# A two-layer network in one kernel: TensorE's instructions of the recurrence in an order written by hand

## The chip, the core and the metric

The kernel runs on one core of a Trainium2 chip. The time is that of one execution on the device, in microseconds (us), from the first to the last instruction of the program and what lies around them; smaller is better. The engines are TensorE (PE in the profile, with its weight loads as PEld), VectorE (DVE), ScalarE (ACT), GpSimd (POOL) and SyncE (SP), whose queue issues nearly all DMAs.

## The reference

The input is two sequences of 1024 tokens of 256 values, in float32. Each block's result is added to its input and a layer norm follows:

```python
x = _layernorm(x + _L0_attn_ref(x, ...))   # causal attention with rope, 32 query heads, 8 key heads
x = _layernorm(x + _L0_ffn_ref(x, ...))    # gated FFN with int8 weights, 1024 hidden
x = _layernorm(x + _L1_attn_ref(x, ...))   # gated delta rule, 16 heads of 128
x = _layernorm(x + _L1_ffn_ref(x, ...))    # FFN with weights sign(w), relu, 1024 hidden
```

The change touches the third line. There q, k and v are each a projection, a causal convolution over four tokens and a SiLU, and a state S of 128 x 128 per head goes from token to token:

```python
def step(S, inp):
    qt, kt, vt, at, bt = inp
    err = jnp.einsum('bhvk,bhk->bhv', S, kt) - vt
    S = at[..., None, None] * S - bt[..., None, None] * err[..., None] * kt[:, :, None, :]
    o = jnp.einsum('bhvk,bhk->bhv', S, qt)
    return (S, o)
```

Then o is normalised per head, multiplied with sigmoid(x @ Wg), and projected with Wo.

## The kernel before

Attention and most of the first FFN fill the first 690 us or so. The third line is done by `delta_rule`, with the rest of the first FFN at its start and the last FFN at its end.

**Units.** The 2048 tokens are four halves of 512 (`hi`), each in four chunks of 128 (`c`). The 16 heads are eight pairs (`s`). A *unit* `i` is one pair of heads in one half; there are 32. Inside a chunk the recurrence is solved at once: a triangular matrix `lt` of each chunk is inverted ahead, and then only the step from chunk to chunk is serial.

**Parts of a unit**, each a Python generator that writes some instructions and then yields a weight:

- `keys(i)` (four units ahead): projection of k for each of the two heads (`project`, six matmuls into one of the two banks of the PSUM pool `ps_p`; `mm3`, lines 790 to 792), the convolution `conv` (bias on ScalarE, L209; three terms on VectorE, L216; SiLU, L223), the scan of the decay (L247) and k times k (`pkk`, L253, into `lt`, L254).
- `blocks(n)` (for two units at once): forward substitution of the 16 x 16 diagonal blocks in 15 steps of two VectorE instructions (L297, L300), a copy (L302), a write to DRAM and eight loads back (L310), a transpose on VectorE (L313).
- `levels(n)`: the inverse is built up from blocks of 16 to 32, 64 and 128 by small matmuls (`p0`, `px`, `p1`, `p2`, `p3`, `p4`: lines 325 to 380), each with a copy on VectorE or ScalarE to the next.
- `others(i)` and `rest_of(i)` (one unit ahead): q and v as k above, the transpose of k (`pk`, L395, to `kc`, L397), k times q (`pkq`, L404, L405), decays multiplied in on GpSimd (L416, L417), and the projection and tanh of the gate (L422).
- `recur(i)`: the chain. Per chunk: `pr` (L517, L521), copied to `prs` on ScalarE (L523); `pw` (L529), copied to `wc` (L531); `pm` (L541), from which VectorE makes the next state `M` (L547, L545), that the next `pr` needs; and `po` (L554, L555), copied to `o` (L558).
- `finish(i - 1)` (the tail): normalise o (L438 to L452), transpose it (`pt`, L458, into the one bank of the pool "t"), gate it (L460, `y` L461), split it on GpSimd (L464, L740), project it (`pf`) and add it to the tokens (L478).
- `last_ffn`, from unit 29 on: the last FFN (L619 to L658), matmuls `ph` (L633, L634) and `po` (L644).

**Order.** `merge` takes, for each unit, the parts that belong to its stage, and always goes on with the one whose yielded weights are least, as a share of the part's total (`KEYS`, `OTHERS`, `RECUR`, ...). What is written so is not yet the order on the engines: a scheduler goes through the program with its own model of times, and gives each engine the ready instruction that was written first; only dependencies are kept. `blocks` is written whole at the start of its stage, and a step of the tail follows each step of the chain.

Of the kernel before, what the change touches and what calls it, by code (L numbers as in the profile page):

```python
# [20 lines left out]
P = 128  # L21
# [10 lines left out]
HP = 2  # L32
# [51 lines left out]
KEYS, OTHERS, FIRST_OTHERS, RECUR, GATES, LEVELS, TAIL = 9.685, 11.658, 15.197, 12.328, 3.1, 24.4, 1.711  # L84
FFN0, FFN1, FFN1_LAST, FFN1_TAIL = 15.0, 2.0, 8.0, 1.0
LEVEL_STEPS = 7.0, 1.5, 1.5, 3.0, 1.7, 2.7, 0.509, 2.908


def delta_rule(
    tc, a, w1d, xs, ident, load_tokens, store_tokens, mm3, sub_low, rsqrt, layernorm, open_pool, gx, gates, halves,  # L90
    before, out, up_scale, down_scale,
# [111 lines left out]
    def conv(m, i, h, bufs):  # L203
# [3 lines left out]
        pp = project(m, i, h)  # L207
# [18 lines left out]
    def keys(i):  # L226
# [6 lines left out]
        dec = [decay(hi, s * HP + h, 0, "da") for h in range(HP)]  # L233
        for h in range(HP):
            conv("k", i, h, 10)
            if h == 0 and i < last:
                st[i + 1]["wk"] = weights("k", place(i + 1)[1])
            yield 1.3
        for h in range(HP):
# [11 lines left out]
            for c in range(HC):  # L251
                t = slice(c * P, (c + 1) * P)
                nc.tensor.matmul(pkk[:, t], lhsT=k[:, t], rhs=k[:, t], start=True, stop=True)  # L253
# [4 lines left out]
            yield 1.1  # L258
# [17 lines left out]
    def blocks(i, psum):  # L276
# [16 lines left out]
        for j in range(SB - 1):  # L293
# [7 lines left out]
            yield 0.3  # L301
# [14 lines left out]
    def levels(i, psum):  # L316
# [5 lines left out]
        with tc.high_priority():  # L322
            for v in range(2 * U):
                for r in quarter:
                    nc.tensor.matmul(p0[r, v, :], lhsT=lo[r, v, :], rhs=dd[r, v, :], start=True, stop=True)
# [6 lines left out]
        with tc.high_priority():  # L332
            for v in range(2 * U):
                for r in quarter:
                    nc.tensor.matmul(px[r, v, :], lhsT=dt[r, v, :], rhs=n0[r, v, :], start=True, stop=True)
# [13 lines left out]
        with tc.high_priority():  # L349
            for v, lt, u in us:  # L350
                nc.tensor.matmul(p1[b1, v, :], lhsT=lt[b0, u, b1], rhs=X[b0, v, 0:BL], start=True, stop=True)
                nc.tensor.matmul(p1[b3, v, :], lhsT=lt[b2, u, b3], rhs=X[b2, v, 0:BL], start=True, stop=True)
# [5 lines left out]
        with tc.high_priority():  # L358
            for v, lt, u in us:
                nc.tensor.matmul(p2[b0, v, :], lhsT=n1[b1, v, :], rhs=lt[b1, u, b1], start=True, stop=True)  # L360
                nc.tensor.matmul(p2[b1, v, :], lhsT=lt[b1, u, b1], rhs=n1[b1, v, :], start=True, stop=True)
                nc.tensor.matmul(p2[b2, v, :], lhsT=n1[b3, v, :], rhs=lt[b3, u, b3], start=True, stop=True)
# [6 lines left out]
        for n in range(2):  # L369
            p3 = bank(*psum, "p3").rearrange("p (u t) -> p u t", t=64)  # L370
            with tc.high_priority():
                for v, lt, u in us[n * U : (n + 1) * U]:
                    nc.tensor.matmul(p3[Z, u, :], lhsT=lt[A, u, Z], rhs=X[A, v, :], start=True, stop=True)
# [4 lines left out]
            with tc.high_priority():  # L378
                for v, lt, u in us[n * U : (n + 1) * U]:
                    nc.tensor.matmul(p4[A, u, :], lhsT=n3[Z, u, :], rhs=lt[Z, u, Z], start=True, stop=True)  # L380
# [3 lines left out]
    def others(i):  # L384

        for m in "qv":
            for h in range(HP):
                conv(m, i, h, 4)
                yield 1.3
        for h in range(HP):  # L390
            e, k, q = st[i]["at", h], st[i]["k", h], st[i]["q", h]
            pk = bank(ps_m, "m", "pk")
            for c in range(HC):
                t = slice(c * P, (c + 1) * P)
                nc.tensor.transpose(pk[:, t], k[:, t], ident)  # L395
# [4 lines left out]
            st[i]["kc", h] = kc  # L400
            pkq = bank(ps_m, "m", "pkq")
            for c in range(HC):
                t = slice(c * P, (c + 1) * P)
                nc.tensor.matmul(pkq[:, t], lhsT=k[:, t], rhs=q[:, t], start=True, stop=True)  # L404
            nc.vector.scalar_tensor_tensor(e, pkq, -SCALE, e, ALU.mult, ALU.mult)  # L405
            yield 1.3

    def rest_of(i):
# [4 lines left out]
        for h in range(HP):  # L413
# [4 lines left out]
            yield 0.2  # L418
        for h in range(HP):
            pp = project("g", i, h)  # L420
            g = half_tile(pools["late"], "gt", 5)
            nc.scalar.activation(g, pp, AF.Tanh, scale=0.5)  # L422
            st[i]["gt", h] = g
            yield 1.3

    def finish(i, wo, o, chunks):
# [26 lines left out]
        yield 0  # L453
        ys = []
        for h in range(HP):
            pt = bank(pools["t"], "t", "pt")[:, 0 : nc_ * P]
            for c in chunks:
                nc.tensor.transpose(pt[:, (c - c1) * P : (c - c1 + 1) * P], o[:, c, h, :], ident)  # L458
# [8 lines left out]
            yield 0.45 * nc_ / HC  # L467
        for c0 in range(0, nc_, 2):
            pf = bank(pools["t"], "t", "pf").rearrange("p (c e) -> p c e", e=E)
            for c in range(2):  # L470
# [4 lines left out]
                if c == 0:  # L475
                    yield 0.87
# [5 lines left out]
            yield 0.87  # L482
# [5 lines left out]
    def recur(i):  # L488
# [13 lines left out]
        def tail():  # L502
            while tails:
                w = next(tails[0], None)
                if w is not None:
                    return w
                tails.pop(0)
            return 0.0

        lt = st[i]["lt"]  # L510
        o = pools["late"].tile([P, HC, HP, P], F32, name="o", tag="o")
        for c in range(HC):
            t = slice(c * P, (c + 1) * P)
            pr = bank(pools["c"], "c", "pr")
            for h in range(HP):
                r = slice(h * P, (h + 1) * P)
                nc.tensor.matmul(  # L517
                    pr[:, r], lhsT=st[i]["v", h][:, t], rhs=ident, start=True, stop=(M is None), is_transpose=True
                )
                if M is not None:  # L520
                    nc.tensor.matmul(pr[:, r], lhsT=st[i]["k", h][:, t], rhs=M[:, r], start=False, stop=True)  # L521
            prs = pools["late"].tile([P, HP * P], F32, name="prs", tag="prs")
            nc.scalar.copy(prs, pr[:, 0 : HP * P])  # L523
            yield 0.65
            yield tail()
            pw = bank(pools["c"], "c", "pw")
            for h in range(HP):
                r = slice(h * P, (h + 1) * P)
                nc.tensor.matmul(pw[:, r], lhsT=lt[:, h * HC + c, :], rhs=prs[:, r], start=True, stop=True)  # L529
            wc = pools["late"].tile([P, HP * P], F32, name="wc", tag="wc")  # L530
            nc.scalar.copy(wc, pw[:, 0 : HP * P])  # L531
            yield 0.45
            yield tail()
            Mn = None
            if hi % 2 == 0 or c < HC - 1:
# [3 lines left out]
                for h in range(HP):  # L539
                    r = slice(h * P, (h + 1) * P)  # L540
                    nc.tensor.matmul(pm[:, r], lhsT=st[i]["kc", h][:, c, :], rhs=wc[:, r], start=True, stop=True)  # L541
# [9 lines left out]
            for h in range(HP):  # L551
                r = slice(h * P, (h + 1) * P)
                if M is not None:
                    nc.tensor.matmul(po[:, r], lhsT=st[i]["q", h][:, t], rhs=M[:, r], start=True, stop=False)  # L554
                nc.tensor.matmul(  # L555
                    po[:, r], lhsT=st[i]["at", h][:, t], rhs=wc[:, r], start=(M is None), stop=True
                )
# [4 lines left out]
            yield 1.3  # L562
            yield tail()
# [7 lines left out]
    def last_ffn():  # L571
# [29 lines left out]
        for j, (hi, c0, nc_) in enumerate(pieces):  # L601
# [10 lines left out]
            for n in range(0, nc_, 2):  # L612
# [4 lines left out]
                for k in range(2):  # L617
                    for i in range(2):
                        nc.tensor.transpose(  # L619
                            pt[:, k, i * P : (i + 1) * P], x[:, c0 + n + i, k * P : (k + 1) * P], ident  # L620
                        )
# [6 lines left out]
            for f in range(NF + 1):  # L628
                if f < NF:
                    ph = bank(ps_p, "p", "ph")[:, w_]  # L630
                    for k in range(2):
                        w = up[2 * k + f // 4][:, f % 4 * P : (f % 4 + 1) * P]
                        nc.tensor.matmul(ph, lhsT=w, rhs=xh[:, k, w_], start=(k == 0), stop=False)  # L633
# [816 lines left out]
```

## Time and profile before

| | |
|---|---|
| median of three timed runs | 2095.18 us (2093.09 to 2097.55) |
| profiled execution | 2099.4 us |
| its span | 2097.7 us |
| matmuls busy | 1905.9 us, 91% |
| weight loads busy | 1498.2 us, 71% |
| VectorE busy | 1611.1 us, 77% |
| ScalarE busy | 1131.9 us, 54% |
| GpSimd busy | 762.8 us, 36% |
| mean granted TensorE clock | 0.973 |

The span runs from the first to the last instruction; the 1.7 us beside it lie around the program. "Busy" is the time that an engine's instructions cover. Matmuls overlap, so that a new one starts before the last has ended, and a busy TensorE may still have room. Records of fp32 matmuls come as two passes each. A line of the profile names the engine, the line of the kernel, and the tile written and those read.

### The profile page before, as it was taken

To read this page: it belongs to the slowest core of one execution; us is meant where nothing else is said; L and a number is where in the kernel's file an instruction comes from. 1 tells how busy PE (TensorE), PEld (TensorE's weight loads), DVE (VectorE), ACT (ScalarE), POOL (GpSimd) and SP (SyncE) were. 2 spreads that over 40 slices of the span, in tenths; PEclk is the share of its full clock that TensorE was granted. 3 is DMA by queue.
4 is the path that set the end of the run, shared out by engine and by line. 5 is a ranking of instruction groups with operands and counts; after the bars stand their busy time and mean duration, and the time that the engine had idled before them with its cause. 6 is when DMAs were issued, how large, how long until landed. Compare 5 with 4: busy or idle time off the path is not lost.

```text
span 2097.7 us, 48705 instructions
## 1 busy us (share of the span) xinstructions
PE 1905.9 (91%) x18656; PEld 1498.2 (71%) x18656; DVE 1611.1 (77%) x3878; ACT 1131.9 (54%) x2349; POOL 762.8 (36%) x1217
## 2 busy tenths in 40 slices
PE   4989999999988887899999999999999999999996
PEld 2545555555555786788888888888888888787885
DVE  5756666877747996587788878888898888978587
ACT  2355566576655345555555555655564565555543
POOL 1243333331123322144363443444345344344331
PEclk9899999999999899999999999999999999999999
DMA  7454443442132421443444444443444343443110
GB/s 222 144 164 144 144 131 126 142 134 68 51 75 61 133 64 35 127 126 91 119 121 115 124 118 115 107 120 107 121 131 119 113 118 107 137 118 107 32 41 31
DMA packets 313514, 230.90 MB, mean 110 GB/s; under 512 B 139649, under 2 KB 278657, under 8 KB 313281
## 3 DMA queue, kind: packets, MB, share of 16 engines
q1 hardware_dynamic: 299472, 210.80, 34.6%
q10 hardware_dynamic: 9632, 10.76, 1.6%
q0 software_dynamic: 4176, 6.23, 1.2%
q8 instruction: 147, 2.41, 0.5%
q14 instruction: 87, 0.70, 0.1%
HBM read 172.95 MB, written 51.87 MB: 107 GB/s over the span
## 4 chain that ended last, share of the span: by engine, by line
PE 50%; DVE 19%; ACT 6%; DMA 5%; issue 4%; SPq 1%; POOL 1%; POOLq 0%; DVEq 0%; ACTq 0%
PE pp L790 4%; PE pp L792 4%; PE pp L791 4%; PE ps L1110 4%; PE av L1131 3%; PE ps L1058 3%; DVE q L216 2%; PE pkq L404 2%; DVE at L247 2%; PE pw L529 2%; PE pm L541 2%; DVE k L216 2%; PE pkk L253 2%; PE po L555 2%; PE p L380 2%
## 5 line engine op out<-in xcount | busy, mean ns | idle before, releaser
L1067 DVE TENSOR_REDUCE mx<-ps 128x4 f32<-128x1024 f32 (+1 forms) x320 | 344.7, 1111 | 133.5 <-PE ps L1058 91.9
L1114 ACT ACTIVATE es<-ps 128x512 f32<-128x512 f32 (+1 forms) x608 | 314.8, 577 | 135.3 <-PE ps L1110 128.7
L1110 PE MATMUL ps<-qT,kT 128*128 128x512 f32 (+3 forms) x768 | 221.1, 369 | 17.9 <-ACT es L1114 15.8
L1058 PE MATMUL ps<-kT,qT 128*128 128x512 f32 x576 | 203.2, 428 | 23.3 <-DVE mx L1067 16.9
L1110 PEld LDWEIGHTS ps<-qT,kT 128*128 128x128 f32 x768 | 130.9, 189 | 106.2 <-ACT es L1114 53.7
L216 DVE SCALAR_TENSOR_TENSOR k<-pp,cw,k 128x511 f32<-128x511 f32 (+2 forms) x192 | 141.8, 740 | 31.0 <-ACT k L209 19.9
L1058 PEld LDWEIGHTS ps<-kT,qT 128*128 128x128 f32 x576 | 102.5, 194 | 85.7 <-DVE mx L1067 51.9
L1131 PE MATMUL av<-es,vaug 128*32 128x512 f32 (+3 forms) x1536 | 161.7, 501 | 0.0
L216 DVE SCALAR_TENSOR_TENSOR v<-pp,cw,v 128x511 f32<-128x511 f32 (+2 forms) x192 | 141.2, 738 | 13.1 <-ACT halos L213 8.5
L416 POOL TENSOR_TENSOR q<-q,dg 128x512 f32<-128x512 f32 x64 | 82.2, 1285 | 184.5 <-ACT pt L460 31.6
L216 DVE SCALAR_TENSOR_TENSOR q<-pp,cw,q 128x511 f32<-128x511 f32 (+2 forms) x192 | 139.2, 733 | 11.0 <-ACT q L209 9.4
L740 POOL TENSOR_TENSOR wfl<-wf,wfh 128x256 fp32r<-128x256 f32 x80 | 58.4, 733 | 208.3 <-ACT wfh L828 165.2
L1117 POOL TENSOR_SCALAR_AFFINE_SELECT es<-es 128x512 f32<-128x512 f32 x128 | 80.3, 636 | 146.9 <-ACT es L1114 146.7
L529 PE MATMUL pw<-prs,lt 128*128 128x128 f32 x512 | 84.8, 288 | 23.4 <-ACT prs L523 23.3
L555 PE MATMUL po<-wc,at 128*128 128x128 f32 x512 | 98.4, 279 | 2.1 <-ACT wc L531 1.2
L763 POOL TENSOR_TENSOR om<-om 128x8 f32<-128x8 f32 x93 | 20.3, 218 | 213.7 <-DVE om L756 113.8
L529 PEld LDWEIGHTS pw<-prs,lt 128*128 128x128 f32 x512 | 70.7, 194 | 33.2 <-ACT prs L523 29.7
L558 ACT COPY o<-po 128x256 f32<-128x256 f32 x128 | 47.6, 372 | 79.3 <-PE po L555 78.4
L242 POOL TENSOR_SCALAR_AFFINE_SELECT d<-col 128x512 f32<-128x512 f32 x64 | 51.2, 812 | 105.6 <-DVE at L247 96.7
L554 PE MATMUL po<-M,q 128*128 128x128 f32 x448 | 87.6, 278 | 0.0
L828 ACT CAST wfh<-wf 128x256 fp32r<-128x256 f32 x80 | 32.3, 406 | 101.6 <-DMA wf<-in_w1k 28.6
L531 ACT COPY wc<-pw 128x256 f32<-128x256 f32 x128 | 47.5, 371 | 72.7 <-PE pw L529 71.7
(305 smaller groups left out, 5646.1 us busy)
## 6 DMA issues: line engine op xcount, KB each, us to landing
da<-dec SPq DMA_DIRECT2D x64, 256.0 KB
wk<-w1k SPq DMA_DIRECT2D x64, 256.0 KB
wq<-w1q SPq DMA_DIRECT2D x64, 256.0 KB
wv<-w1v SPq DMA_DIRECT2D x64, 256.0 KB
dg<-dec SPq DMA_DIRECT2D x64, 256.0 KB
wg<-w1g SPq DMA_DIRECT2D x64, 256.0 KB
wo<-w1o SPq DMA_DIRECT2D x64, 256.0 KB
ad<-avs ACTq DMA_DIRECT2D x32, 256.0 KB
```

Of the source, the lines that this page charges most:

```text
L216: nc.vector.scalar_tensor_tensor(acc[:, d:], pp[:, 0 : HT - d], cw[:, n, hd, KS - 1 - d : KS - d], acc[:, d:], ALU.mult, ALU.add)
L529: nc.tensor.matmul(pw[:, r], lhsT=lt[:, h * HC + c, :], rhs=prs[:, r], start=True, stop=True)
L554: nc.tensor.matmul(po[:, r], lhsT=st[i]["q", h][:, t], rhs=M[:, r], start=True, stop=False)
L555: nc.tensor.matmul(po[:, r], lhsT=st[i]["at", h][:, t], rhs=wc[:, r], start=(M is None), stop=True)
L790: nc.tensor.matmul(out, lhsT=lhi, rhs=rhi, start=k0, stop=False)
L791: nc.tensor.matmul(out, lhsT=lhi, rhs=rlo, start=False, stop=False)
L792: nc.tensor.matmul(out, lhsT=llo, rhs=rhi, start=False, stop=k1)
L1058: anchor["mm"] = nc.tensor.matmul(ps[:, j - j0, :].rearrange("p (g k) -> p g k", k=P), lhsT=q_, rhs=kT[:, :, j * P : (j + 1) * P], start=T ...
L1067: nc.vector.tensor_reduce(mx[:, it, j0 // 2, :], ps[:, 0:n, :].rearrange("p j (g k) -> p g j k", k=P), AX.XY, ALU.max)
L1110: nc.tensor.matmul(ps[:, g - g0, :], lhsT=kT[:, g, jb * P : (jb + 1) * P], rhs=qT[:, i0 : i0 + w], start=True, stop=True,)
L1114: exps.append(nc.scalar.activation(es[:, g0 : g0 + n, 0:w], ps, AF.Exp, scale=D ** -0.5))
L1131: mm = nc.tensor.matmul(av[ROW * g : ROW * (g + 1), i0 - ih * 512 : 512], lhsT=vaugs[b][:, jb, kv, :], rhs=es[:, g, 0:w], start=(jb == 0), ...
```

## The change

TensorE's instructions are linked, each to the one before, by a dependency that costs no semaphore, from unit 0 on; so TensorE runs them in the order in which they were written. All weights are now shares of a stage, set so that each step of a part comes at a chosen place. `merge` keeps the chain apart: after a step of it, at least four instructions of TensorE from other parts are written before its next one, if there are any. Both heads are projected one right behind the other, before their convolutions. `pk` comes ahead of q and v in `others`. The tail is a part of its own, and `blocks` too, its 15 steps spread over the stage.

```diff
-KEYS, OTHERS, FIRST_OTHERS, RECUR, GATES, LEVELS, TAIL = 9.685, 11.658, 15.197, 12.328, 3.1, 24.4, 1.711
-FFN0, FFN1, FFN1_LAST, FFN1_TAIL = 15.0, 2.0, 8.0, 1.0
-LEVEL_STEPS = 7.0, 1.5, 1.5, 3.0, 1.7, 2.7, 0.509, 2.908
+GATES, TAIL = 3.1, 0.4
+FFN0, FFN1, FFN1_LAST, FFN1_TAIL = 7.6, 2.0, 8.0, 1.0
+LEVEL_STEPS = 0.2, 0.1, 0.04, 0.15, 0.075, 0.13, 0.045, 0.08
+class InLine:
+    def __init__(self, tc):
+        self.tc, self.strict, self.last, self.count = tc, False, None, 0
+    def link(self, made):
+        if self.strict and self.last is not None:
+            self.tc.add_manual_dep(
+                made.ins, self.last.ins.name,
+                mybir.DependencyInfo(mybir.DependencyClass.NoSync, mybir.DependencyReason.DATA), reason="order",
+            )
+        self.last = made
+        self.count += 1
+        return made
...
     def keys(i):
...
+        yield 0.04
+        pps = [project("k", i, h) for h in range(HP)]
+        if i < last:
+            st[i + 1]["wk"] = weights("k", place(i + 1)[1])
         for h in range(HP):
-            conv("k", i, h, 10)
-            if h == 0 and i < last:
-                st[i + 1]["wk"] = weights("k", place(i + 1)[1])
-            yield 1.3
+            conv("k", i, h, 10, pps[h])
+        yield 0.36
...
     def blocks(i, psum):
...
-            yield 0.3
+            yield 0.06
...
     def others(i):
-        for m in "qv":
-            for h in range(HP):
-                conv(m, i, h, 4)
-                yield 1.3
+        yield 0.12
         for h in range(HP):
...
+        yield 0.15
+        for m in "qv":
+            pps = [project(m, i, h) for h in range(HP)]
+            for h in range(HP):
+                conv(m, i, h, 4, pps[h])
+            yield 0.25 if m == "q" else 0.17
...
     def rest_of(i):
...
+        yield 0.04
+        pps = [project("g", i, h) for h in range(HP)]
         for h in range(HP):
-            pp = project("g", i, h)
...
     def recur(i):
...
             nc.scalar.copy(prs, pr[:, 0 : HP * P])
-            yield 0.65
-            yield tail()
+            yield 0.09
...
             nc.scalar.copy(wc, pw[:, 0 : HP * P])
-            yield 0.45
-            yield tail()
+            yield 0.08
...
-            yield 1.3
-            yield tail()
+            yield 0.08
...
-    def merge(parts, aside=None):
+    def merge(parts, aside=None, chain=None):
...
+        held = None
+        if chain:
+            chain = [*chain, 0.0, True]
+            parts.append(chain)
         while any(p[3] for p in parts):
-            p = min(parts, key=lambda p: p[2] / p[1])
+            free = [p for p in parts if not (p is chain and held is not None and te.count < held + 4)]
+            p = min(free or parts, key=lambda p: p[2] / p[1])
...
+            if p is chain:
+                held = te.count
...
     for i in range(-AHEAD, last + 1):
+        te.strict = i >= 0
...
         if n % 2 == 1 and 3 <= n <= last:
-            drain(blocks(n - 1, (pools["l"], "l")))
+            parts.append((blocks(n - 1, (pools["l"], "l")), 1.0))
...
+        if i >= 0 and tails:
+            parts.append((rest(), 1.0))
...
-        merge(parts, aside)
-    for t in tails:
-        merge([(t, TAIL)], (ffn1, FFN1_TAIL))
+        merge(parts, aside, (recur(i), 1.0) if i >= 0 else None)
+    merge([(rest(), TAIL)], (ffn1, FFN1_TAIL))
```

Every `nc.tensor.matmul` and `nc.tensor.transpose` is passed to `te.link`; `rest()` runs the tails that are open. The weights of `finish` are shares now too, and two of its yields are gone.

## The prediction

> **What bounds the kernel now.** I read the page's head first, then the table by stages, then the list of waits, then the timeline around one drop of the clock. All times are those of the profiled execution: 2099.4 us, of which the span is 2097.7; the three timed runs have a median of 2095.2, so a saving is taken off both alike.
>
> The page's head, share of the span and the granted clock:
>
> ```profile
> PE 1905.9 (91%) x18656; PEld 1498.2 (71%) x18656; DVE 1611.1 (77%) x3878; ACT 1131.9 (54%) x2349; POOL 762.8 (36%) x1217
> ...
> PEclk9899999999999899999999999999999999999999
> ```
>
> TensorE leads, VectorE is second, and the two stand close. The first `prs` copy (L523) of unit 1 starts at 887.0 us and that of unit 28 at 1897.2: 27 units in 1010.2 us, a pitch of 37.4 us. The change keeps TensorE's order up to about 830 us almost as it was, so those 32 units (some 1200 us) and the last FFN behind them are all that it can move. Two units out of the table by stages (a line is: stretch, its length, busy time of PE, PEld, DVE, ACT, POOL, clock, DMA share, GB/s), and the sum over units 1 to 20:
>
> ```profile
> 1373.90:1411.00 37.10, 35.14 (x536) 31.09 (x534) 30.61 (x76) 21.52 (x46) 17.21 (x30) 1.00 0.43 119
> 1411.00:1446.80 35.80, 35.14 (x361) 31.61 (x362) 29.15 (x83) 19.54 (x46) 14.02 (x25) 1.00 0.43 117
> ...
> sum 749.50, PE 708.38 PEld 625.32 DVE 620.23 ACT 418.84 POOL 320.56; mean PE 35.42 PEld 31.27 DVE 31.01 ACT 20.94 POOL 16.03
> ```
>
> A unit has 35.4 us of busy TensorE and 31.0 of busy VectorE in 37.5. Starts show more room than "busy" does: in the chain of waits 128x512 projections start 0.233 us apart, 128x128 passes 0.112, transposes 0.109, 128x256 passes 0.118. A unit's 48 projections, 107 passes, 24 transposes and 24 `pf` make 11.2 + 12.0 + 2.6 + 2.8 us, and half of a pair's substitution levels some 4.2 (four groups of 1.07 and some 4 us of smaller ones in each pair): an estimate of 32.8 us. So no order makes a unit shorter than about 33 us; VectorE's 31 us lie just below.
>
> What TensorE waited for between 900 and 1930 us (27.5 units), total, times, longest:
>
> ```profile
> PE pw L529 <- ACT prs L523: 14.0, 23, 1.6
> PE pm L541 <- ACT wc L531: 9.3, 20, 0.7
> PE pp L790 <- DVE q L216: 7.1, 12, 1.4
> PE p L373 <- ACT lt L368: 4.0, 4, 1.6
> PE p L360 <- ACT n L356: 3.9, 4, 2.5
> PE pr L517 <- DVE M L547: 3.3, 1, 3.3
> PE pp L790 <- DVE k L216: 3.2, 5, 0.9
> ```
>
> All rows of this list make 55 us, 2.0 us a unit, 64 us over 32 units. That is the pot. The two first rows are the chain: `pr` to `prs` to `pw`, `pw` to `wc` to `pm`, each with a 0.372 us copy on ScalarE between.
>
> **The change, part by part.** Counts of instructions are the same on every engine: 12,318 matmuls are written in both. Only places change.
>
> *Chain steps at fixed places.* In the new order, 12 projections (12 x 0.233 = 2.8 us) stand between most `pr` and their `pw`. The need is the last pass 0.275 + copy 0.372, and at worst one bias activation ahead in ScalarE's queue (L209, 0.78): 1.4 us. So the 14.0 us go. Between `pw` and `pm` stand 8 transposes (0.87), one `pkk` (0.90) or 12 `pf` (1.4 us), against the same 0.65 to 1.4: half of 9.3 + 1.2 (the `po` row on `wc`) goes, 5.2. That is 19.2 us over 27.5 units, 22 over 32. If the cover were gone, the old 1.0 us a unit would be back.
>
> *Substitution spread.* The 15 steps (L297, L300: 41.4 + 43.2 us for 14 pairs of units, 6.0 us a pair) no longer stand at the head of a stage but between the convolutions. `p1` to `p2` now has `pr` and a projection pair between (3.5 us) against two `n1` of 0.59 behind eight copies of 0.40; `p2` to `p3` has 4.1 us against 0.68 + 4 x 0.36. So the 4.0 and 3.9 us go: 9 us over 32 units. What may be late next is the step after it: the last row is copied (L302), then written out and read back by eight loads on SP's queue; that chain took 8.7 us once (1229.6 to 1238.3), and the new order leaves 11.7 us from the `g` projections to `p0` (2.8 + `pw` 0.45 + `pf` 1.41 + `po` 0.9 + `pr` 0.67 + 2.8 + `pw` 0.45 + `pk` 0.87 + `pm` 0.45 + `po` 0.9). SP's queue holds the same loads, in some pairs with `wo`, which waits for `pf`, among the eight. 3.0 us of cover: I take nothing, and at worst the same 3.0 for each of 14 pairs (+42).
>
> *Both heads' projections together.* Two PSUM banks hold them. The second head's six matmuls come 1.4 us after the first's, and wait until VectorE has done the third convolution term of the previous pair's second head. In VectorE's new order there stand, between the two third terms, in an even unit: `kc` 0.68, two `M` 0.68, a `k` term 0.74, two statistics 0.56, three normalisations 1.16 and the last term 0.74: 4.6 us of durations. So the wait may be up to 4.6 - 1.4 = 3.2 us where VectorE is behind. Below, all the present 10.3 us (`pp` on `q` and `k`) could go, -12 over 32 units; above, 3.2 in each of 16 even units, +51. The nearest row is the present wait for the same bank, 0.6 us at a time: I take no change, 0.
>
> *Fixed places behind VectorE.* `pt` of the second head waits for the only bank of its pool, that is for `y` of the first (L461), which VectorE's queue holds behind the `q` convolution. Between the two `pt` stand 2.7 us of TensorE's work; the need is 0.75 (L460) + 0.68, or, if all six terms of 0.74 are still ahead, 4.4 + 0.7. Below, the present 1.1 us goes, -1; above, 4.4 + 0.7 - 2.7 = 2.4 us a unit, +77. Nearest row: 1.1 us in 27.5 units; with nothing to pull ahead I take 0.1 a unit, +3.
>
> *The last FFN.* A block is four `ph` and four `po` (L644), 8 x 0.233 = 1.86 us. In the new order the `po` of a block stand right behind the next four `ph` (0.93 us), and need relu 0.69 + copy 0.53 + difference 0.93 = 2.15 after their own. Taken by turns this gives (1.86 + 2.15) / 2 = 2.0 us a block, 0.15 more; with POOL's difference (1.28) 2.18, 0.32 more. About 20 such blocks stand behind the chain: +3; below 0, above +6. 54 more of its matmuls (12.6 us) stand behind the chain's end than now; the last three units lose the same work.
>
> Sum: -22 - 9 + 0 + 3 + 3 = -25 us. Profiled 2099.4 - 25 = 2074; median 2095 - 25 = **2070**.
>
> Two rules of the Trainium skill bear on this. The trace has a clock of 0.50 in stretches of 3.4 or 6.8 us; one:
>
> ```profile
> 1486.00:1492.70 6.70, 4.61 (x42) 4.06 (x41) 6.61 (x19) 3.71 (x10) 0.00 (x0) 1.00 0.69 220
> 1492.70:1499.50 6.80, 6.80 (x29) 5.26 (x29) 4.10 (x22) 2.19 (x5) 2.32 (x12) 0.50 0.25 81
> ```
>
> It came when TensorE had been busy 4.61 of 6.70 us, with one wait of 1.6 in it; a stretch costs half its length, 3.4 us. "TensorE: Matmul & The Clock Gate", Part 1 (the HAM clock gate), says that the clock falls to half after an idle window of some 3.4 us; the row shows it after less. By the rule, waits of at most 3.2 us would cost no clock; by the row, one in each pair of units would cost up to 14 x 3.4 = 48 us more, which speaks against the change. Second, "Trainium Kernel Development and Optimization", Performance Expectations, calls busy matmul time a bad measure and LDWEIGHTS time a good one: here 625.3 of 749.5 us, so by it 17% of a unit, 200 us over 32, would be room; the list of waits has 64.
>
> **Rivals.** *Slower: in-order TensorE behind VectorE.* Everything behind a waiting matmul waits too, and the scheduler no longer pulls other work ahead. For it: VectorE's 31 us in a unit of 33, and the bank wait of 3.2 us above. Against: in the present order the same banks cost 10 us in all. If it strikes in the 16 even units, 16 x 3.2 = 51 us, less 31 saved, +6 of the two small terms: +26, about 2121. It decides from 31 / 32 = 1 us a unit.
> *Large gain.* All 64 us of waits go, and VectorE's 31 us stay hidden: 2095 - 64 = 2031; against it, VectorE then would be busy 31 of 35.4.
> *No change.* The waits only change their names: the chain's 1 us a unit returns as waits for banks. 2095.
>
> **How the numbers follow.** Chances: forecast 0.40 (2050 to 2085), large gain 0.18, no change 0.08 (within 0.2%, 4 us, about what a measurement can tell here), slower 0.34. Faster 0.58. The range takes in the large gain with a little of the half clock's return (2020) and the slower case with a part of both upper bounds (51 + 77, half of it, less 31): 2128, so 2130. What lies above needs both at once, or SP's 42 us.
>
> **What the new profile would show.** Right: the rows of `pw` on `prs` and `p` on `n` and `lt` gone, a pitch near 36.6 us, VectorE at 31 us a unit. Wrong: `pp` waiting for L216 or `pt` for `y` by more than 30 us in all, the clock at 0.50 more often than now (five stretches between 900 and 1930), or VectorE waiting for the loads of `dt`.

## The result, and the profile after

The changed kernel takes 2206.3 us (median of four runs, 2197.6 to 2208.1), the kernel before beside it 2096.3 us: a ratio of 1.0519, interval 1.0488 to 1.0550. The forecast of 2070 us and its range up to 2130 us were wrong. The profiled execution took 2208.1 us, its span is 2206.4.

Line numbers have moved: the convolution's term L216 is now L232, the projections L790 to L792 are L817 to L819, `pt` L458 is L482, `y` L461 is L485, the chain's copies L523 and L531 are L537 and L544, the substitution's L297 is L316 and the copy into its bank L292 is L311. The head of the page after:

```profile
PE 1937.2 (88%) x18656; PEld 1515.4 (69%) x18656; DVE 1596.7 (72%) x3878; ACT 1144.6 (52%) x2349; POOL 760.8 (34%) x1217
...
PEclk8999999999998998999999999999989999999998
```

The work is the same. TensorE is busy 31 us longer than before, and the span is 109 us longer, so most of the loss is TensorE standing still. Cut at the first `prs` copies of units 0 and 28, it divides so:

| stretch | before, us | after, us | loss | TensorE idle, before and after |
|---|---|---|---|---|
| span's start to unit 0 | 836.5 | 846.6 | 10.1 | |
| unit 0 to unit 28 | 1060.7 | 1110.8 | 50.1 | 63.7, 107.2 |
| unit 28 to the end | 200.5 | 249.0 | 48.5 | 23.7, 49.3 |

In the middle, what TensorE waited for between 880 and 1960 us (total, times, longest):

```profile
PE pp L817 <- DVE k L232: 53.0, 33, 2.5
PE pt L482 <- DVE y L485: 15.4, 12, 3.2
PE pr L535 <- DVE M L557: 9.1, 8, 2.9
PE pr L535 <- DVE M L559: 7.4, 7, 2.2
PE pm L553 <- ACT wc L544: 5.1, 7, 0.9
PE pw L542 <- ACT prs L537: 2.1, 2, 1.4
```

The two rows that led before, 14.0 and 9.3 us on ScalarE's copies, now stand at the foot with 2.1 and 5.1. Above them are new rows, all on VectorE. The largest, a projection that waits for a bank which the key convolution still reads, had 3.2 us in the list of before.

The table by stages shows where. An odd stage (unit 17's), then an even one (unit 18's), columns as in the prediction:

```profile
1509.00:1554.90 45.90, 41.32 (x681) 36.02 (x680) 31.54 (x87) 25.84 (x58) 13.85 (x24) 0.96 0.48 134
1554.90:1590.00 35.10, 31.25 (x206) 28.14 (x205) 30.35 (x92) 16.77 (x38) 14.57 (x25) 0.95 0.43 113
```

Stages are no longer alike. An odd one has the levels of a pair of units (681 matmul records against 206), an even one the substitution on VectorE. Over units 2 to 27 TensorE is busy 41.4 us in an odd stage and 30.7 in an even one, at 45.3 and 34.7 us a stage; before it was 35.9 and 35.0, at 37.9 and 37.4. VectorE is busy 31.1 and 30.6 us of a stage. In all gaps of over 0.15 us ahead of `pp` from 846 to 1957 us (55.3 us), 48.4 lie in even stages, nearly all at two places, 6.7 and 10.6 us after the stage's start. Both seen in TensorE's timeline of unit 18, in brackets the idle time before an instruction:

```profile
1559.39 0.61 PE L567 MATMUL po<-wc,at 128*128 128x128 f32 x4
1561.73 0.50 PE L817 MATMUL pp<-x2h,wq 128*128 128x512 f32 x1 [1.73 <-DVE k L232]
...
1565.52 0.50 PE L817 MATMUL pp<-x2h,wq 128*128 128x512 f32 x1 [2.12 <-DVE k L232]
```

The two heads' query projections each wait for the bank of a key projection, and with a written order nothing may go ahead of them.

VectorE's own waits, in the same stretch, are led by one that was 4.3 us before:

```profile
DVE tmp L316 <- ACT pi L311: 110.6, 14, 9.5
DVE v L232 <- ACT halos L229: 20.5, 14, 5.5
```

Once in each pair of units, near the end of the odd stage, VectorE stands some 8 us at the first substitution step, and nothing that is queued behind that step runs meanwhile. The step's bank is the one of the levels, and ScalarE's copy into it comes behind the last level's copy. 110 us look like the whole loss; the first experiments are about that.

At the end, TensorE's longest wait is at a transpose of the heads' outputs. In GpSimd's timeline (first two lines) a difference of the last FFN comes first, then 12 small steps (3.4 us together), then the normalisation; in TensorE's (last two) the wait:

```profile
2031.70 1.26 POOL L767 TENSOR_TENSOR slt<-stt,slt 128x512 fp32r<-128x512 f32 x1 [10.09 <-DVE om L783]
...
2036.47 2.42 POOL L476 TENSOR_SCALAR o<-o,om 128x128 f32<-128x128 f32 x3
```

```profile
2030.05 0.39 PE L645 MATMUL ph<-swk,sk 128*128 128x512 f32 x1
2037.38 0.90 PE L482 MATMUL pt<-ident,o 128*128 128x128 f32 x3 [6.94 <-POOL o L476]
```

During that wait, at 2034.0 us, the clock falls to 0.50 and stays there for 17.1 us. From 820 us on it is there 23 times, 133 us in all; before, 8 times and 54 us.

The stretch from unit 28 to the end as a whole, before (first line) and after:

```profile
1897.20:2097.70 200.50, 176.84 (x1518) 149.81 (x1518) 153.13 (x531) 92.50 (x186) 71.74 (x108) 0.97 0.16 49
1957.40:2206.40 249.00, 199.67 (x1532) 163.06 (x1530) 153.77 (x530) 95.87 (x188) 71.92 (x108) 0.90 0.14 44
```

### The profile page after: what moved, and what is told of

The parts are those of the page before. It is cut to its first block, busy times and chain, and to the rows that moved or that the text cites. A ratio compares the mean times of both kernels' runs of the same rounds, so it can differ in the third digit from the quotient of the medians.

```text
span 2206.4 us, 48736 instructions
## 1 busy us (share of the span) xinstructions
PE 1937.2 (88%) x18656; PEld 1515.4 (69%) x18656; DVE 1596.7 (72%) x3878; ACT 1144.6 (52%) x2349; POOL 760.8 (34%) x1217
## 4 chain that ended last, share of the span: by engine, by line
PE 46%; DVE 25%; DMA 5%; ACT 4%; issue 4%; POOL 2%; SPq 2%; DVEq 0%; ACTq 0%; POOLq 0%
DVE k L232 5%; PE av L1158 4%; PE ps L1137 4%; PE pp L817 4%; PE pp L819 3%; PE pp L818 3%; PE ps L1085 3%; DVE at L265 3%; PE pkk L271 2%; PE pkq L428 2%; PE pr L535 2%; DVE q L232 2%; DVE kc L413 2%; PE p L399 2%; DVE v L232 1%
## 5 line engine op out<-in xcount | busy, mean ns | idle before, releaser
L232 DVE SCALAR_TENSOR_TENSOR v<-pp,cw,v 128x511 f32<-128x511 f32 (+2 forms) x192 | 138.2, 743 | 42.2 <-ACT halos L229 21.6
L232 DVE SCALAR_TENSOR_TENSOR q<-pp,cw,q 128x511 f32<-128x511 f32 (+2 forms) x192 | 140.7, 739 | 16.0 <-ACT halos L229 7.7
L232 DVE SCALAR_TENSOR_TENSOR k<-pp,cw,k 128x511 f32<-128x511 f32 (+2 forms) x192 | 140.3, 739 | 14.9 <-ACT halos L229 13.5
L488 POOL CAST yh<-y 128x512 fp32r<-128x512 f32 x62 | 38.1, 614 | 275.9 <-DVE y L485 225.4
L316 DVE TENSOR_TENSOR tmp<-pi,ll 128x15 f32<-128x15 f32 (+7 forms) x240 | 47.1, 196 | 112.3 <-ACT pi L311 110.6
L817 PE MATMUL pp<-x2h,wq 128*128 128x512 f32 x128 | 61.3, 479 | 56.7 <-DVE k L232 55.3
L535 PE MATMUL pr<-M,k 128*128 128x128 f32 x448 | 88.5, 293 | 19.7 <-DVE M L559 9.4
L535 PEld LDWEIGHTS pr<-M,k 128*128 128x128 f32 x448 | 74.7, 209 | 26.0 <-DVE M L559 11.3
```

The source lines that it names most:

```text
L232: nc.vector.scalar_tensor_tensor(acc[:, d:], pp[:, 0 : HT - d], cw[:, n, hd, KS - 1 - d : KS - d], acc[:, d:], ALU.mult, ALU.add)
L535: te.link(nc.tensor.matmul(pr[:, r], lhsT=st[i]["k", h][:, t], rhs=M[:, r], start=False, stop=True))
L817: te.link(nc.tensor.matmul(out, lhsT=lhi, rhs=rhi, start=k0, stop=False))
```

## The experiments

Ratios are to the kernel before, measured beside each run, with 95% intervals; the change itself has 1.0519. The expectations name theories; the first is that VectorE's stand at the substitution is the loss, its rivals that TensorE's written order costs by itself. Run 6 decides whether the order is the cause; the others ask where it costs.

**1. Substitution in SBUF** (on the changed kernel)

```diff
-        wide = bank(*psum, "pi")[:, 0 : SB * SB].rearrange("p (c r) -> p c r", r=SB)
-        nc.scalar.copy(wide, tt)
+        wide = tt
...
-        nc.scalar.copy(tt, wide)
```

> The changed kernel, but the substitution works in its SBUF tile in place of a PSUM bank: the ScalarE copies into and out of the bank and the bank itself are gone, so that VectorE's first substitution step waits for no ScalarE copy. Theory one (VectorE, which takes its instructions in order, stands at the first substitution step, 110.6 us in 14 times, until the bank of the levels comes free): those waits go, odd stages fall from 42 to 51 us to under 40, units 0 to 28 take 1050 to 1070 us in place of 1111, the kernel 2130 to 2165 us. Theory two (TensorE in written order waits by itself for banks behind VectorE, 53 us before the projections): VectorE only reaches its next wait sooner, odd stages stay over 42 us, the kernel stays over 2185 us. Either way nothing is expected of the stages behind unit 28 (249 us).

Measured: 2244.5 us, 1.0694 (1.0663 to 1.0725), slower still. VectorE's waits now begin with another row, while TensorE's first row (second fence) stays as it was:

```profile
DVE xtok L498 <- PE pf L817: 54.0, 19, 4.6
```

```profile
PE pp L815 <- DVE k L232: 56.7, 33, 3.1
```

The 110 us are gone, and odd stages take 47.1 us instead of 45.3. VectorE only comes sooner to the next instruction that waits for TensorE, as theory two said. But the run is not clean: in SBUF the steps themselves became slower (told at the end), and VectorE is busy 38.4 us of an odd stage instead of 31.1. So it speaks against theory one and does not settle it; runs 2, 8, 9 and 13 bear on it too.

**2. First substitution step behind the key convolution**

```diff
+            if j == 0 and te.strict:   # order only: behind the last convolution term written
+                tc.add_manual_dep(first.ins, te.conv.ins.name, NoSync)
...
-            yield 0.06
+            yield 0.056   # the steps begin one yield of 0.06 later and stand closer together
```

> The changed kernel, its substitution in PSUM as it was, but from stage 0 on VectorE may take the first step only behind the key convolution of the same stage (an order between two VectorE instructions, no wait on another engine), so that the two scans, the state's updates and the key convolutions no longer stand behind a step that waits for its bank; the other steps stand a little closer together, so that the last ends where it did. Theory H: VectorE's hold makes the key convolutions late and TensorE, in written order, waits 48 us for them in the even stages: that wait falls under 20 us and the kernel to 2145 to 2180 us. If VectorE's load in those stages, not the hold, makes them late (as the run with the substitution in SBUF suggests, where the hold was gone and the wait stayed at 57 us), the wait stays over 40 us and the time within 12 us of 2206.

Measured: 2244.8 us, 1.0697 (1.0673 to 1.0720). TensorE's two first rows:

```profile
PE pp L824 <- DVE k L232: 42.7, 27, 2.1
PE p L351 <- DVE ll L339: 35.4, 11, 7.9
```

VectorE's stand is one row of 7.9 us, and it stands 124.8 us at `xtok` for `pf` instead. The key row keeps 42.7 us, and the levels' first matmul is now late, as the substitution ends late. So with the steps in PSUM, without run 1's slowness, the key row still stays over 40 us, which was to speak against the theory. The 38 us over the changed kernel were not expected. VectorE's idle time looks like a consequence: near the end of odd stages it stands, at one instruction or another, until TensorE gets there.

**3. Substitution in one piece again**

```diff
-            parts.append((blocks(n - 1, (pools["l"], "l")), 1.0))
+            drain(blocks(n - 1, (pools["l"], "l")))
```

> The changed kernel, but the substitution is issued as one piece at the head of its stage again, as in the kernel before; all else as changed. If spreading as such costs (a step that waits between two convolutions), the time falls to under 2150 us. Theory one (the first step stands ahead of its bank's release): the first step keeps its place in VectorE's order, so 90 to 120 us of waits for the copy into the bank remain, and the time stays within 15 us of 2206.

Measured: 2226.6 us, 1.0612 (1.0589 to 1.0635): 0.9% over the change's ratio. Spreading is worth some 19 us within the written order; it isn't what costs. The first step's wait stays (101.1 us), as theory one expected; the 15 us were a little exceeded.

**4. Projections head by head**

```diff
-        pps = [project("k", i, h) for h in range(HP)]
...
+            conv("k", i, h, 10, project("k", i, h))   # q, v and g likewise
```

> The changed kernel, but each projection is issued head by head, a unit's second head behind the first head's convolution, as before; weights of the places kept. Theory three (the pairs of projections hold both banks, and TensorE waits for VectorE to clear them): the 53 us before the projections fall under 25 and the time by 20 to 40 us. Theory one (those waits only pass on VectorE's hold at the first substitution step): the wait for the copy into the bank stays near 110 us and the time within 12 us of 2206.

Measured: 2183.5 us, 1.0396 (1.0365 to 1.0427), 23 us better; the key row falls from 53.0 to 30.9 us and not under 25. The pairs are a part of the loss while the order is fixed.

**5. The end free**

```diff
-        te.strict = i >= 0
+        te.strict = 0 <= i < START   # START = 29; also off for the tails
```

> The changed kernel, but TensorE's order is bound to the written one only in stages 0 to 28; from stage 29 on (the last units, the tails and the last feed-forward) the scheduler orders it, as before. Stages from unit 28's start to the end took 249 us changed and 200.5 before. If the written order costs there (feed-forward matmuls at fixed places between links of the chain that wait for VectorE and ScalarE, with the clock at half for 48 us of it), the end comes back to 200 to 220 us and the time falls by 30 to 50 us. If the order of issue alone does it, or the feed-forward's weight 8 in the last stage, it stays over 240 us.

Measured: 2171.2 us, 1.0341 (1.0310 to 1.0372), 35 us better; the end from unit 28 takes 208.4 us instead of 249.0.

**6. All free: the change without the order**

```diff
-        te.strict = i >= 0
+        te.strict = False
```

> The changed kernel with its places, pairs and spread substitution, but TensorE's order is left to the scheduler in every stage. Theory A: the written order keeps each stage's TensorE work inside its stage, so that odd stages (with the levels of the inverses: TensorE busy 41.4 of 45.3 us) wait on TensorE and even ones (30.7 of 34.7 us) on VectorE, where the kernel before had 35.0 of 37.4 and 35.9 of 37.9. Left to the scheduler, TensorE's busy time per stage is level again within 2 us, odd and even stages differ by under 4 us, and the kernel takes 2085 to 2130 us. Theory B: the places, pairs and the spread cost by themselves, in any order: odd stages stay over 42 us and the kernel over 2160 us.

Measured: 2099.5 us, 1.0006 (0.9988 to 1.0024). The whole loss is gone, with all places, pairs and the spread substitution kept. What TensorE waited for here, between 880 and 1960 us:

```profile
PE pm L553 <- ACT wc L544: 12.5, 27, 0.7
PE pw L542 <- ACT prs L537: 9.1, 19, 1.0
PE pp L817 <- DVE k L232: 5.6, 10, 0.9
```

The chain's two waits are back, and the key row is gone. But theory A's picture was wrong in one point: stages are still unequal, 43.3 and 32.2 us, TensorE busy 40.6 and 30.4. So inequality alone costs nothing; the sum of a pair is 75.5 us, as before (75.2), and 80.0 with the order. What differs is TensorE's idle time: 4.5 us a pair free, 7.8 bound.

**7. The order alone, on the kernel before**

```diff
+        te.strict = 0 <= i < START   # and te.link(...) around each matmul of the kernel before
```

> The kernel before, with its own weights, single projections and substitution in one piece, but TensorE bound to the order in which its instructions are written, in stages 0 to 28 (the last stages and the tails are free as before). Theory A: the order alone parts the stages: TensorE's busy time per stage differs by 8 us or more between odd and even, odd stages take over 42 us, and the kernel 2130 us or more. Theory B (the order is free, the new places cost): odd and even stages stay within 4 us, the kernel within 20 us of 2100.

Measured: 2474.5 us, 1.1758 (1.1722 to 1.1795); stages of 57.5 and 44.9 us; 85.2 us of TensorE's time go at `pt` alone, on GpSimd's normalisation, and from 820 us on the clock is at half for 387 us. With the same stages bound, the new places make 2474 into 2171 us (run 5). They are good places for a written order; the free order is better.

**8. The gate's projections of even units moved to the even stage**

```diff
+        if i % 2 == 0 and 0 < i < last:
+            parts.append((gate(i), 0.23))   # and left out of rest_of(i)
```

> The changed kernel, TensorE in written order, but the output gate's projections of the even units, written at the end of the odd stages, are written at the head of the next, even stage (12 matmuls of 512 columns, some 4 us of TensorE, from the odd stages to the even ones; their weights are loaded no later). Theory A: the odd stages shorten by 2.5 to 4 us each, the even ones lengthen by less, as the moved matmuls fill the 48 us for which TensorE waits for the key convolution there: 2160 to 2195 us. If VectorE's order sets the pace of both stages, the odd stages stay at 45 us and the time within 8 us of 2206.

Measured: 2214.4 us, 1.0520 (1.0476 to 1.0564): nothing. Even stages take 1.0 us more, odd ones 0.2 less; the key row keeps 56.7 us and has single waits of up to 4.0. The moved matmuls did not fill the waits, they stood in front of them. VectorE's stand at the first substitution step fell here from 110.6 to 65.4 us, and no time was gained by it.

**9. The edits of runs 4, 5 and 8 together**

> The changed kernel with three things together: projections head by head again, TensorE free from stage 29 on, and the gate's projections of even units moved to the even stages. If the three costs stand side by side (23 us and 33 us as their single runs showed, and 10 to 30 us for the move), the kernel takes 2110 to 2140 us, still behind the kernel before, as odd and even stages remain unequal by 4 us or more; if the pairs and the move pay for the same waits, 2140 to 2155 us.

Measured: 2114.6 us, 1.0060 (1.0038 to 1.0082). The gains of runs 4 and 5 would add up to 2148 us; some 33 us more came with the move, which was worth nothing with pairs. No run has the move with single projections alone, so what brings them is not shown. Odd stages take 42.6 us, even ones 34.1. Units 0 to 28 take 1062.7 us, nearly the 1060.7 of the kernel before, though VectorE still stands 54.8 us at the first substitution step: one more row against theory one. This is the best bound version, still behind the kernel before.

**10. Run 9, bound from stage 1, and the first step behind the key convolution**

```diff
-        te.strict = 0 <= i < START
+        te.strict = 1 <= i < START   # and run 2's edit
```

> The kernel with head-by-head projections, the gate's projections of even units in the even stages and a free TensorE from stage 29 on (2114.6 us), with two edits more: the first substitution step behind the key convolution, and TensorE's order bound from stage 1 on in place of stage 0, so that the first stage's chain does not stand behind the gate's projections that wait 13.3 us for their weights (unit 0 starts at 846 us, against 836 in the kernel before). Theory H: 8 to 10 us from the start and 10 to 25 us from the waits for the key convolution (30 us there): 2078 to 2098 us, at or ahead of the kernel before. Without H: only the start's 8 to 10 us, 2103 to 2108 us.

Measured: 2230.8 us, 1.0639 (1.0614 to 1.0664). Unit 0 starts at 834.2 us as expected, but the levels' first matmul now waits 80.5 us for the substitution in nine odd stages. As in run 2, a later step is paid for by what needs it.

**11. The query pair of even stages written later**

```diff
-        yield 0.15
+        yield 0.27 if i % 2 else 0.15   # i is the unit, one ahead of its stage
...
-            yield 0.25 if m == "q" else 0.17
+            yield (0.2 if m == "q" else 0.1) if i % 2 else 0.25 if m == "q" else 0.17
```

> The changed kernel with one place moved: in the even stages, which have no levels between the key projections and the query projections, the query pair is written 12 hundredths of a stage (about 4 us) later, and the value pair's and the gate pair's distances shortened by as much. Theory D: the shares of a stage are right for odd stages, whose 10.7 us of levels stand between the pairs, and too near in even ones, so that TensorE meets the query pair before the key convolution has given back its bank (48 us of the 55): that wait falls under 25 us, the kernel to 2165 to 2192 us. If VectorE's load is what makes the even stages (busy 30.6 of 34.7 us), the wait moves to the value pair, the state or the heads' outputs, and the time stays within 10 us of 2206.

Measured: 2235.9 us, 1.0661 (1.0638 to 1.0684). TensorE's first rows, and the key row:

```profile
PE pt L482 <- POOL o L476: 32.0, 14, 3.4
PE pt L482 <- ACT o L473: 18.6, 13, 1.8
...
PE pp L817 <- DVE k L232: 5.9, 7, 1.3
```

The wait left the query pair, as theory D said, and went to the transposes of the heads' outputs, now the next in the order: 49.7 us in even stages, at 7.3 to 9.8 us from their start. So the query pair's place alone is not at fault: what comes next in the order finds its operand unfinished as well. The rival was right on where the time goes, though not on the size (30 us worse).

**12. Only the chain bound**

```diff
-                te.link(nc.tensor.matmul(pw[:, r], ...))
+                te.bind(nc.tensor.matmul(pw[:, r], ...))   # all of recur; other matmuls free
```

> The changed kernel, but of TensorE's instructions only those of the recurrence's chain are bound, each behind the instruction that is written ahead of it (stages 1 to 28); projections, levels and all other work are left to the scheduler. If the order is worth something only between the chain's links: the waits for the two copies of the chain (21.6 us when the whole order is free) fall under 12 us, those before the projections stay under 15, and the kernel takes 2075 to 2095 us, ahead of the kernel before. If a link that is bound behind work which waits for VectorE makes the chain late, 2110 us or more.

Measured: 2229.4 us, 1.0634 (1.0612 to 1.0657). The chain's waits do not fall (17.3 us for `wc` and 16.2 for `prs`, against 12.5 and 9.1 in run 6). The reading is that a link behind another instruction inherits that one's wait, and the whole chain with it; no run shows that by itself.

**13. Even stages bound alone, odd ones alone**

```diff
-        te.strict = i >= 0
+        te.strict = 1 <= i < START and i % 2 == 0   # 1 for the second
```

> The changed kernel with TensorE bound to the written order only in the even stages from 2 to 28 (keys, substitution on VectorE, no levels); odd stages, the start and the end are free. If the loss is made in the even stages themselves, where TensorE finds its next written operand unfinished (48 us before the query pair, or before the transposes of the heads' outputs when that pair is later), it stays: 2130 to 2165 us. If it is made in the odd ones, whose order leaves VectorE idle and hands its work on to the next stage: 2085 to 2110 us.

> The changed kernel with TensorE bound to the written order only in the odd stages from 1 to 27 (with the levels); even stages, the start and the end are free. If the loss is made in the even stages themselves: 2085 to 2110 us, with the chain's two waits in odd stages under 4 us. If it is made in the odd ones (VectorE idle before the substitution's first step, its work late in the next stage): VectorE's wait for the copy into the bank stays over 80 us and the time at 2130 to 2170 us.

Measured: 2135.2 us, 1.0174 (1.0152 to 1.0196), and 2190.7 us, 1.0436 (1.0412 to 1.0460). Either kind costs when it is bound alone, the odd ones more. With these bound VectorE stood 5.9 us at the substitution's first step, not 80. But it stood all the same, late in the odd stages, at instructions whose operands come from TensorE, directly (`pk`) or by way of ScalarE. Its three first rows, between 880 and 1960 us:

```profile
DVE k L232 <- ACT k L225: 57.7, 10, 8.8
DVE kc L413 <- PE pk L411: 24.8, 8, 4.2
DVE k L232 <- ACT halos L229: 24.2, 4, 8.8
```

So VectorE stands whether or not the substitution's bank holds it. The two runs do not divide the loss: with odd stages alone bound, units 0 to 28 take 1146.4 us, more than the 1110.8 with all bound. Free stages give work away to bound ones: TensorE is busy 50.3 us in an odd stage and 22.8 in an even one.

**14. The start**, run 9 with `te.strict = 1 <= i < START`

> The kernel with head-by-head projections, the gate's projections of even units in even stages and a free TensorE from stage 29 on (2114.6 us), bound from stage 1 on in place of stage 0. The chain of unit 0 then no longer stands behind the gate's projections that wait 13.3 us for their weights: unit 0 starts at 834 to 838 us in place of 846, and the kernel takes 2103 to 2108 us; that is the part of the start in the loss. If the later stages take it up, it stays at 2112 to 2117 us.

Measured: 2115.1 us, 1.0077 (1.0052 to 1.0102). Unit 0 starts at 832.3 us, 13.5 earlier, and units 0 to 28 take 14.2 us more, with the clock at half for 115 us in place of 79. The start is a wait on the profile and no part of the loss that could be taken back alone. Why it comes back later was not settled.

**15. The end bound alone, and single projections in a free order**

```diff
-        te.strict = i >= 0
+        te.strict = i >= START   # for the first; False, with run 4's edit, for the second
```

> The changed kernel with TensorE bound to the written order only from stage 29 to the end, free before. If the bound end costs by itself what freeing it gave back (33 to 35 us; 249 against 208 us from unit 28's start), the kernel takes 2128 to 2145 us and the end 235 to 250 us. If the end was only late because the stages ahead of it left it a worse state, the end stays under 215 us and the time within 12 us of 2100.

> The changed kernel with TensorE free in all stages and the projections issued head by head. In written order that gave 23 us. If pairs cost only because TensorE must wait for their banks in a fixed order, nothing is left to gain when the order is free: within 6 us of 2099.5. If a pair costs in any order, 2075 to 2090 us, which would be ahead of the kernel before.

Measured: 2153.1 us, 1.0243 (1.0207 to 1.0279), the end at 247.3 us in the profiled execution, which was the fastest (2139.3). The end costs by itself, 41 to 54 us over run 6, more than was expected. And 2106.2 us, 1.0034 (1.0019 to 1.0048): where TensorE is free, pairs cost nothing; single projections are even some 6 us behind run 6. Pairs cost only where the order is fixed.

## Why the prediction was wrong

*Chain steps at fixed places* (forecast -22, which is 19.2 for the list's 27.5 units): right in mechanism, nearly in size. The three rows, 14.0, 9.3 and 1.2 us, became 2.1, 5.1 and none: 17.3 us less. (Taken from unit 0 on, the rows on `prs` and `wc` lose 22.4 us, but there one wait of 8.8 us at unit 0 helps, which the sum did not hold.) Run 6 is the counterproof: without the order the two waits return (21.6 us). (All rows of the list, the pot, add up to 57 us and not 55; the terms do not rest on that.)

*Substitution spread* (forecast -9): the sign was right. The rows of `p` on `n` and `lt` fell from 8.6 to 1.9 us, and run 3 puts the spread at some 19 us. The new row that I had not seen coming, VectorE's 110.6 us at the first step, is real, but the loss does not go with it (runs 2, 8, 9 and 13). It was the tempting explanation, and wrong.

*Both heads' projections together* (forecast 0, bounds -12 to +51): this is the step that failed first. The working had found the wait: VectorE's queue between two third terms, up to 3.2 us in each of 16 even units. Then I took 0, because the present wait for the same bank was 0.6 us at a time. That row was measured in a free order, in which the scheduler puts other work ahead of a projection whose bank is busy; it says nothing of an order in which it may not. The change measured 55.3 us against 11.7 on `q` and `k` in the same stretch before, a loss of 43.6; 48.4 of the 55.3 lie in even stages. That this is near my upper bound (51) is in part luck: the term had one wait, of the second head, and the trace has two in each even stage, of up to 1.8 us for the first head (19.8 us in all) and 2.5 for the second (28.6).

*Fixed places behind VectorE* (forecast +3, bounds -1 to +77): the same fault, a row of 1.1 us from the free order. It measured 15.4 us, and a third of the kind that I had not listed, `pr` waiting for the state `M`, rose from 3.3 to 16.5.

*The last FFN* (forecast +3, 0 to +6): mis-sized and wrongly bounded. I counted the latency inside the FFN's blocks and left out that one late instruction of the last units' tails holds the whole of TensorE, the FFN with it. Unit 28 to the end takes 48.5 us more, 25.6 of it more idle time and 22.8 longer busy for the same work, at a clock of 0.90 instead of 0.97. The longest wait, 6.9 us, is for a normalisation on GpSimd; the FFN's difference ahead of it took only 1.3 us of that. The other waits are many and short, and which of them costs most stays open. Run 15 shows that the bound end costs this by itself. With the pairs this is the largest miss of the sum, and it lies wholly outside its bounds. For the start's 10.1 us the sum had no term at all.

*The clock*: the row that was weighed there spoke truly. A wait of 1.73 us and one of 2.12 were enough in unit 18; the stretch with them, and the next (granted clock third from the end):

```profile
1559.60:1566.40 6.80, 2.95 (x14) 2.01 (x13) 6.80 (x23) 3.24 (x7) 3.92 (x11) 1.00 0.31 82
1566.40:1569.80 3.40, 3.40 (x15) 3.01 (x14) 3.23 (x10) 1.65 (x4) 0.00 (x0) 0.50 0.36 114
```

I named +48 us for it and put none of it into the sum. (Stretches of 0.50 are not only 3.4 or 6.8 us long: before, there is one of 13.7 us around the start of unit 0 and one of 9.7 at the end.)

*The rival "slower"* had the mechanism, the place (even units) and the size of its main term; it was given 0.34 and 2121 us, for it counted the 51 us of waits for banks alone and had nothing for the end and the start. My range ended at 2130 us because I thought that only both upper bounds at once, or SP's queue, could pass it; the 50 us of units 0 to 28 pass it alone, and the end adds as much again. The signs that I named for being wrong (waits of `pp` and `pt` over 30 us, more drops of the clock) all came.

What stays open: how the 50 us of units 0 to 28 divide between even and odd stages, since binding either moves work into it; how much of the loss the clock is, since no run had the waits without the drops; and which waits at the end cost most.

## What to carry to other kernels

A list of waits taken in a free order gives what an order by hand may gain (here 17 of the 19 us came), not what it costs: the price is made of latencies that the scheduler steps round and the list does not show, so weigh the worst case of each queue, and of each other engine that an instruction waits on, in place of the present row. When one engine's wait as large as the whole loss appears, take it away before believing it, and look where the engine stands then. And try the new places without the order first: here that run (run 6) beside the changed kernel told the order's price, and that the places alone bring nothing.

## What the runs showed of the hardware

In run 1 the substitution steps, two float32 inputs in SBUF, took 207 ns in the mean, and 227 at most, when no GpSimd instruction ran beside them (387 of 480), and 507 in the mean when one did (93), up to 1.28 us for one. In the changed kernel, with one of the two inputs in PSUM, the same steps took 199 and 200 ns, beside GpSimd (205) or not (275). The copy into a bank, which looks like waste, so protects these steps. The Trainium skill, "SBUF — State Buffer", section "Who interferes with whom", says that a VectorE instruction with two SBUF inputs contends with a GpSimd instruction that reads SBUF. It says too that one with at most one SBUF input, outside the modes that use two ports, does not. The numbers here agree with both.
